# Layer 1's shared weights joined to the scaled mask by an accumulating DMA instead of VectorE

## The chip, the cores and the metric

The kernel runs on one core of a Trainium2 chip, in one launch. The time is device microseconds of the core; five runs of the kernel before gave a median of 629.24 us (628.68 to 630.3). A profile of one further execution of it is shown below.

## The reference

Eight batches of 256 tokens with 1024 features pass four layers, each added to its input. All data is float32, the masks are int32.

```python
# layer 0: a shared weight and a mixture of 8 experts of rank 16 (top 2 of the logits)
base = jnp.einsum('btd,od->bto', x, W)
...
return base + SCALING * lora_out
# layer 1: a shared weight W, a bias, and a signed mask of its own for each batch
output = jnp.einsum('bsi,oi->bso', hidden_states, W) + b
sign = (2 * mask - 1).astype(hidden_states.dtype)
diff = jnp.einsum('bsi,bio->bso', hidden_states, sign)
return output + diff * coeff[:, None, None]
# layer 2: one of 8 full weights, chosen by the batch's adapter
w = weight[adapter_ids]
return jnp.einsum('bsi,boi->bso', x, w)
# layer 3: one of 8 adapters of rank 16
...
x = x + _L0_cond_ref(x, itok_B_0_7, L0_cond_W, L0_cond_Wr, L0_cond_A, L0_cond_B)
x = x + _L1_cond_ref(x, L1_cond_W, L1_cond_b, condB_coeff, mask_Bx4096x4096_ik1)
x = x + _L2_cond_ref(x, L2_cond_weight, itok_B_3_7)
x = x + _L3_cond_ref(x, L3_cond_A, L3_cond_B, itok_B_3_7)
```

What matters here is layer 1. For a batch with coefficient c, its weight is W + c (2 mask - 1), and with the residual W + c (2 mask - 1) + I, where I is the identity. W is the same for all batches, the mask is not.

## The kernel before, in words

**Tiling.** The residual stream is kept transposed, with features on the 128 partitions. A weight of 1024 x 1024 is cut into eight blocks by output feature; a block is a tile of 128 partitions x 1024 elements, 512 KB, and holds all inputs of 128 outputs. Batches go in four pairs, q = 0 to 3. The list `units` is the stream of weight blocks in the order of use: for each pair one block "A" (the experts' first matrix), eight blocks "L0", 16 "L1" (eight outputs m, two batches j) and 16 "L2". So a pair has 41 units.

**Precision.** Each float32 operand is split into two float32r parts, a high and a low one. For a unit of A or L0, `three` multiplies both batches of a pair at once: 24 products of 512 columns (lines 412, 413, 420). For a unit of L1 or L2, `two` multiplies one batch: eight products of the high weight with both parts of x side by side (line 428, 512 columns), and eight of the low weight with the high x (line 436, 256 columns).

**A block's preparation.** `load` brings the block in on SP's queue, `LOAD_AHEAD` = 9 units before its use, into one of `RAW_BUFS` = 10 buffers with the tag "raw" (x's halves and layer 3's matrices take their turn in the same ring). `fold` adds the identity to the 128 x 128 part where inputs and outputs are the same (line 159, VectorE). `prep_hi` casts the block to its high part on ScalarE (line 184), and `prep_lo` subtracts that from the block on VectorE (line 191) for the low part; this happens about `PREP_AHEAD` = 4 units ahead. `LAGS` puts some low parts later around the change from layer 1 to layer 2.

**Layer 1 takes two steps more.** `load` also brings in the shared block w1[m] once for a pair of batches (line 133, a ring of `W1_BUFS` = 3). `merge` turns the int32 mask into 2 c mask - c on ScalarE, in place (line 154). `merge_add` adds the shared block on VectorE (line 174), after having added the identity to the shared block itself (line 159, once for both batches).

**The order of the work is written out by hand.** The program runs `slot(i)` for each unit i. In it: the load of unit i + 9; stores of finished outputs; the evacuation of unit i - 1 from PSUM (ScalarE lines 704, 711, 714; VectorE lines 718, 720); preparation of the units up to i + 4; unit i's products; and at its end the merge for the next slot's `merge_add`. Which unit is merged where stands in `merges`: `MERGE_AHEAD` = (6, 7) units of a pair are merged in the slots before layer 1 (six for the first pair, seven for the others), and the rest are spread over the next 12 slots:

```python
for u in range(2 * K):
    merges[n0 + (u - M if u < M else (u - M) * (2 * K - D) // n)] = n0 + u
```

Each engine runs its instructions in the program's order and waits on semaphores. SP issues all loads and nearly all stores. GpSimd writes a few constants at the start and has nothing to do after that. The products of layers 0 to 2 use four PSUM buffers (tag "mm"), so a buffer is free again only when the evacuation of the unit four earlier is done.

Of the kernel before, what the change touches and what calls it, by code (L numbers as in the profile page):

```python
# [15 lines left out]
P = 128  # L16
NB = 8          # batches
T = 256         # tokens of a batch
K = 8           # blocks of 128 features
E = 8           # experts / adapters  # L20
R = 16          # rank
LOAD_AHEAD = 9  # weight blocks loaded, and prepared, ahead of their products
PREP_AHEAD = 4
MERGE_AHEAD = (6, 7)    # layer 1's blocks merged before the layer: the first pair's, the others'
W1_BUFS = 3
RAW_BUFS = 10
WARM = 9        # products that raise the tensor engine's clock
# prepared later, so that the vector engine is free where layer 2 waits for layer 1's results
# [4 lines left out]
def kernel(ctx: ExitStack, tc: tile.TileContext, x, lang, coeff, ids,  # L33
                           mask, w0, wr, la, lb, w1, b1, w2, a3, b3, out):
    """The residual stream is kept transposed (features on partitions), so that each
    layer's output is the next one's moving operand. float32 operands are split
    exactly into two float32r parts (hi: 12 bits, lo: the rest)."""
# [17 lines left out]
    # ---- small constants  # L55
    xraw = {}

    def load_x(b, h, parts=1):
        """Half of batch b's input."""
        t = rawp.tile([P, K // 2, T], F32, tag="raw", name=f"x{b}_{h}")  # L60
        n = K // 2 // parts
        for i in range(parts):
            c = slice(i * n, (i + 1) * n)
            nc.sync.dma_start(t[:, c, :], x[b, :, h * K // 2 + i * n:h * K // 2 + (i + 1) * n, :])
        xraw[b, h] = t

    # the router's weights: 8 columns and 24 of zeros, a quarter of the array's
# [8 lines left out]
    # the sum over the array's quarters, of R rows each, as three copies  # L76
# [11 lines left out]
    # ---- splits  # L88
# [19 lines left out]
    # ---- the stream of weight blocks, in the order of use  # L108
    units = []
    for q in range(NB // 2):  # L110
        units.append(("A", q, 0, 0))
        units += [("L0", q, m, 0) for m in range(K)]
        units += [("L1", q, m, j) for m in range(K) for j in range(2)]
        order = [(m, j) for m in range(K) for j in range(2)]
        if q == NB // 2 - 1:        # the last pair's first batch ends sooner
            order[-6:] = [(m, j) for j in range(2) for m in range(K - 3, K)]
        units += [("L2", q, m, j) for m, j in order]
    raws, ws, w1raw = {}, {}, {}

    def parts(i):  # L120
        # the first blocks come in two parts
        n = 2 if i < 2 else 1
        return [slice(j * K // n, (j + 1) * K // n) for j in range(n)]

    def load(i):
        if i >= len(units):
            return
        kind, q, m, j = units[i]
        b = 2 * q + j
        if kind == "L1":  # L130
            if j == 0:
                w = rawp.tile([P, K, P], F32, tag="w1", name=f"w1_{q}_{m}", bufs=W1_BUFS)
                nc.sync.dma_start(w, w1[m])
                w1raw[q, m] = w
            t = rawp.tile([P, K, P], I32, tag="raw", name=f"raw{i}")
            nc.sync.dma_start(t, mask[b, m])
        else:
            t = rawp.tile([P, K, P], F32, tag="raw", name=f"raw{i}")
            if kind == "A":
                for c in parts(i):  # L140
                    nc.sync.dma_start(t[:, c], la[:, c])
            elif kind == "L0":
                for c in parts(i):
                    nc.sync.dma_start(t[:, c], w0[m][:, c])
            else:
                src = w2[bass.ds(adapter(b), 1), m]
                nc.sync.dma_start(t, src.rearrange("a p k c -> (a p) k c"))
        raws[i] = t

    # a block's preparation in four steps, on two engines in turns  # L150
# [5 lines left out]

    def add_identity(w, m):
        """The residual, in the block where inputs and outputs are the same."""
        nc.vector.tensor_tensor(w[:, m, :], w[:, m, :], ident, ALU.add)  # L159
# [3 lines left out]
    def fold(i):  # L163
        if i < len(units) and units[i][0] in ("L0", "L2") and i not in folded:
            add_identity(raws[i], units[i][2])
            folded.add(i)

    def merge_add(i):
        if i < len(units) and units[i][0] == "L1":
            s = f32(raws[i])  # L170
            _, q, m, j = units[i]
            if j == 0:
                add_identity(w1raw[q, m], m)
            nc.vector.tensor_tensor(s, s, w1raw[q, m], ALU.add)  # L174
# [28 lines left out]
    # first blocks, ahead of the other constants  # L203
# [26 lines left out]
    def constants():  # L230
        # 5 where the expert is the batch's language; ids below 0 match none
# [8 lines left out]
        # adapters as an index: from the end below 0, then held in range  # L240
# [6 lines left out]
    # ---- layer 0's router, from logits [16 = hi|lo, 512 tokens]  # L247
# [4 lines left out]
    def logits(b, h):  # L252
        """Half of batch b's logits in float32, four blocks of features at a time in the
        quarters of the array."""
        q, j = divmod(b, 2)
        if (j, h) == (0, 0):
            pls[q] = aux.tile([P, 512], F32, tag="aux", name=f"pl{q}")
        for g in range(4):
            nc.tensor.matmul(pls[q][32 * g:32 * g + 32, j * T:(j + 1) * T],  # L259
                             wrs[:, 4 * h + g, :], xraw[b, h][:, g, :],  # L260
                             start=(h == 0), stop=(h == 1))
# [11 lines left out]
    def router(q, pt):  # L273
# [31 lines left out]
        # 2 (the scaling) over 1 + e, and e times that  # L305
# [28 lines left out]
    # ---- layer 3, per batch  # L334
# [20 lines left out]
    def proj_sum(b, pb):  # L355
        """The sum over the quarters, three times."""
        pr = aux.tile([P, 512], F32, tag="aux", name=f"pr{b}")
        if b == NB - 1:
            # in one step, as nothing else is left to do meanwhile
# [13 lines left out]
    def third(b, pb):  # L373
        """The projections' rows as hi, lo and hi again."""
# [21 lines left out]
    # ---- products  # L396
# [11 lines left out]
    def three(po, hi, lo, xhi, xlo, last=True, early=(), mid=(), late=()):  # L408
        """po = (hi + lo)^T (xhi + xlo), over the K blocks of 128; early, mid, late:
        other work in between."""  # L410
# [14 lines left out]
    def two(po, hi, lo, xhl, early=(), mid=(), late=()):  # L425
        """As three(), for one batch: hi with x's both parts at once, into po's halves."""
# [21 lines left out]
    summed = []     # units whose two halves' sum is under way  # L448
    done = []       # what is left of the units that have gone through the tensor engine
# [11 lines left out]
    def proj(b, h):  # L461
        """Half of batch b's projections onto its adapter's rank, in float32 and the
        quarters of the array."""
# [14 lines left out]
    def first_products():  # L478
        """The first two units' products and the first logits, as the input comes in."""
# [20 lines left out]
        for j in range(2):  # L500
# [15 lines left out]
            # both halves stay open, for the experts' part, in one group that batch 0 starts  # L516
# [11 lines left out]
    def main(i):  # L528
        """Unit i on the tensor engine."""
# [12 lines left out]
        elif kind == "L0":  # L542
# [12 lines left out]
            if m == 1:  # L555
                def gate_now():
                    gates[q] = gate(gxs.pop(q), phs.pop(q))
                # the first gates come later than the others
# [15 lines left out]
        else:  # L574
# [21 lines left out]
            if i == len(units) - 1:  # L596
                # its sum is waited for at once
                po = po[:, :T]
                three(po, hi, lo, xh[:, :, 0], xh[:, :, 1])
            else:  # L600
                two(po, hi, lo, xh, early=early, mid=mid, late=late)
# [6 lines left out]
    nxt = []        # work for the vector engine once the scalar engine's is done  # L608

    def side(i):  # L610
        """Other loads and preparations beside unit i's products."""
# [19 lines left out]
    # the tensor engine's clock rises while the first blocks come in  # L631
# [8 lines left out]
    # the slots in which layer 1's weights are merged: the more in layer 0's, which leave the  # L640
    # vector engine time
    merges = {}
    for q in range(NB // 2):
        n0 = units.index(("L1", q, 0, 0))
        M = MERGE_AHEAD[min(q, 1)]
        n = 2 * K - M
        for u in range(2 * K):
            merges[n0 + (u - M if u < M else (u - M) * (2 * K - D) // n)] = n0 + u

    def slot(i):  # L650
        """Unit i's products, beside the evacuation of those before it and the
        preparation of those after it."""
# [4 lines left out]
        bulk = nxt[:]  # L657
        nxt.clear()
        ahead = i + min(D, 2 + max(0, i - 2))
        if i in merges:  # L660
            bulk.insert(0, lambda: merge_add(merges[i]))
        if i > 1:
            bulk = bulk[:1] + [lambda: lows(ahead - lag)] + bulk[1:]
# [3 lines left out]
        # the next products wait for the last ones' results: nothing between  # L667
# [28 lines left out]
    def evacuate(between=None):  # L696
        """Products (and bias) split into the next ones' operand."""
        items = done[:]
        done.clear()
        # those summed beside the last unit, then those complete on PSUM  # L700
# [27 lines left out]
    # the last batch's end: half of the residual joins on the tensor engine, so that two  # L728
    # engines can take the sums
# [81 lines left out]
```

## Time and profile before

| | us |
|---|---|
| median of five runs | 629.24 |
| the profiled execution | 628.82 |
| its span, first to last instruction | 627.0 |
| ScalarE: high parts, line 184, 166 of them | 172.4 |
| ScalarE: evacuations and bias in layer 1, line 714, 64 of them | 30.4 |
| SP's own waits, longest in total: line 147 for VectorE's low parts | 129.9 |
| TensorE's granted clock, mean | 0.997 |

The page gives the busy time of each engine in the span. An engine that is busy for less than the span waits in between, and a list of groups of instructions says for each group what ended the idle time just before it. A second view follows the chain of work that ended last back to the start; 98% of it is TensorE. The windows give busy times in a stretch of the span, so that a stage can be read by itself: a pair of batches takes some 152 us, as the first layer-1 units of the pairs start at about 66.8, 219.2, 371.6 and 524.0 us. The DMA rows give the share of time in which the core's 16 DMA engines were busy and what they moved: 125.01 MB in all, at a mean of 199 GB/s.

### The profile page before, as it was taken

The numbers are of one execution on the slowest core, as the hardware profiler recorded it, in microseconds if no ns is written. First come the engines' busy times: TensorE is split into PE (matmuls) and PEld (weight loads), VectorE is DVE, ScalarE is ACT, GpSimd is POOL, SyncE is SP. The second block draws the span as 40 slices with busy tenths as digits, with TensorE's granted clock in tenths as the row PEclk, the third lists the DMA queues.
The fourth block names the chain that finished last, engine by engine and source line by source line (L and its number), as shares of the span: only waits on it lengthen the run. The fifth ranks groups of instructions, "written<-read, shape, count | busy, mean of one in ns | idle before, by whom it ended". The sixth has DMA issues, their size and how long they took to land.

```text
span 627.0 us, 9247 instructions
## 1 busy us (share of the span) xinstructions
PE 618.7 (99%) x3458; PEld 521.8 (83%) x3458; DVE 460.3 (73%) x800; ACT 362.8 (58%) x552; POOL 1.0 (0%) x14
## 2 busy tenths in 40 slices
PE   8999999999999999999999999999999999999996
PEld 6888888888788888888878888888787888888885
DVE  6685898766657799777666689967775678987642
ACT  5375797465354498655435558865534446975521
POOL 0000000000000000000000000000000000000000
PEclk9999999999999999999999999999999999999998
DMA  8974575567625785376842777547774358754104
GB/s 277 392 225 155 202 269 179 202 214 273 238 71 168 221 282 198 138 251 220 320 125 73 205 234 283 188 139 242 241 269 134 123 181 268 245 193 165 38 0 135
DMA packets 38815, 125.01 MB, mean 199 GB/s; under 512 B 4722, under 2 KB 5874, under 8 KB 38770
## 3 DMA queue, kind: packets, MB, share of 16 engines
q1 hardware_dynamic: 38626, 124.15, 58.4%
q8 instruction: 27, 0.44, 0.3%
q10 hardware_dynamic: 144, 0.26, 0.1%
q14 instruction: 18, 0.15, 0.1%
HBM read 116.01 MB, written 8.39 MB: 198 GB/s over the span
## 4 chain that ended last, share of the span: by engine, by line
PE 98%; DMA 1%; SPq 0%; DVE 0%; ACT 0%; DVEq 0%; issue 0%
PE po L428 37%; PE po L436 20%; PE po L412 9%; PE po L420 9%; PE po L413 9%; PE pb L467 1%; PE po L454 1%; PE po L455 1%; PE po L456 1%; PE pl L259 1%; PE po L388 1%; PE ph L420 1%; PE ph L413 1%; PE ph L412 1%; DMA raw<-in_la 1%; PE ph L489 0%
## 5 line engine op out<-in xcount | busy, mean ns | idle before, releaser
L428 PE MATMUL po<-hl,whi 128*128 128x512 f32 x1016 | 254.5, 392 | 0.0
L428 PEld LDWEIGHTS po<-hl,whi 128*128 128x128 f32 x1016 | 182.9, 189 | 32.9
L191 DVE TENSOR_TENSOR wlo<-raw,whi 128x1024 fp32r<-128x1024 f32 (+1 forms) x166 | 198.9, 1204 | 1.8 <-ACT whi L184 1.8
L184 ACT CAST whi<-raw 128x1024 fp32r<-128x1024 f32 (+1 forms) x166 | 172.4, 1039 | 10.8 <-DVE raw L159 8.4
L436 PEld LDWEIGHTS po<-hl,wlo 128*128 128x128 f32 x1016 | 137.7, 190 | 12.2 <-issue 3.3
L436 PE MATMUL po<-hl,wlo 128*128 128x256 f32 x1016 | 142.7, 283 | 0.0
L412 PE MATMUL po<-x0hi,whi 128*128 128x512 f32 x248 | 97.1, 392 | 0.0
L413 PE MATMUL po<-x0lo,whi 128*128 128x512 f32 x248 | 96.7, 390 | 0.0
L174 DVE TENSOR_TENSOR raw<-raw,w 128x1024 f32<-128x1024 f32 x64 | 78.1, 1220 | 3.6 <-ACT raw L154 2.6
L154 ACT ACTIVATE raw<-raw,negc,c 128x1024 f32<-128x1024 int32 x64 | 79.7, 1245 | 0.0
L711 ACT COPY xt<-po 128x256 f32<-128x256 f32 x63 | 23.4, 372 | 87.2 <-PE po L436 87.2
L720 DVE TENSOR_TENSOR xt<-po,xt 128x256 f32<-128x256 f32 x63 | 26.6, 423 | 50.7 <-ACT xt L711 50.4
L420 PE MATMUL po<-x0hi,wlo 128*128 128x512 f32 x248 | 62.3, 393 | 0.0
L704 ACT CAST hl<-po 128x256 fp32r<-128x256 f32 x64 | 20.5, 376 | 71.6 <-PE po L456 71.5
L718 DVE TENSOR_TENSOR hl<-po,hl 128x256 fp32r<-128x256 f32 x64 | 23.8, 419 | 46.1 <-ACT hl L704 40.8
L412 PEld LDWEIGHTS po<-x0hi,whi 128*128 128x128 f32 x248 | 46.6, 188 | 11.1 <-issue 1.2
L413 PEld LDWEIGHTS po<-x0lo,whi 128*128 128x128 f32 x248 | 46.6, 188 | 9.8
L420 PEld LDWEIGHTS po<-x0hi,wlo 128*128 128x128 f32 x248 | 45.4, 188 | 8.8
L714 ACT ACTIVATE sum<-po,b_sb 128x256 f32<-128x256 f32 x64 | 30.4, 475 | 23.5 <-PE po L436 23.2
L720 DVE TENSOR_TENSOR sum<-po,sum 128x256 f32<-128x256 f32 x64 | 26.8, 419 | 12.7 <-ACT sum L714 12.7
L718 DVE TENSOR_TENSOR hl<-sum,hl 128x256 fp32r<-128x256 f32 x64 | 26.8, 418 | 4.6 <-ACT hl L704 4.6
L704 ACT CAST hl<-sum 128x256 fp32r<-128x256 f32 x64 | 25.6, 400 | 7.5 <-DVE sum L720 7.5
(116 smaller groups left out, 379.5 us busy)
## 6 DMA issues: line engine op xcount, KB each, us to landing
raw<-in_w SPq DMA_DIRECT2D x95, 512.0 KB, 4.3
raw<-in_mask SPq DMA_DIRECT2D x64, 512.0 KB, 5.3
w<-in_w SPq DMA_DIRECT2D x32, 512.0 KB, 4.7
out<-xt SPq DMA_DIRECT2D x31, 256.0 KB, 3.0
x<-in_x SPq DMA_DIRECT2D x12, 512.0 KB, 4.7
a3raw<-in_a SPq DMA_DIRECT2D x8, 384.0 KB, 3.6
x<-in_x SPq DMA_DIRECT2D x8, 256.0 KB, 5.5
raw<-in_la SPq DMA_DIRECT2D x3, 512.0 KB, 3.5
```

The source lines that it names most:

```text
L154: nc.scalar.activation(f32(raws[i]), raws[i], AF.Identity, bias=negc[:, b:b + 1], scale=c2[:, b:b + 1])
L174: nc.vector.tensor_tensor(s, s, w1raw[q, m], ALU.add)
L184: nc.scalar.copy(hi[:, c], source(i)[:, c])
L191: nc.vector.tensor_tensor(lo[:, c], source(i)[:, c], f32(ws[i])[:, c], ALU.subtract)
L412: nc.tensor.matmul(po, hi[:, k, :], xhi[:, k, :], start=(k == 0), stop=False)
L413: nc.tensor.matmul(po, hi[:, k, :], xlo[:, k, :], start=False, stop=False)
L420: nc.tensor.matmul(po, lo[:, k, :], xhi[:, k, :], start=False, stop=(last and k == K - 1))
L428: nc.tensor.matmul(po, hi[:, k, :], xhl[:, k].rearrange("p h t -> p (h t)"), start=(k == 0), stop=False)
L436: nc.tensor.matmul(po[:, :T], lo[:, k, :], xhl[:, k, 0, :], start=False, stop=(k == K - 1))
L704: nc.scalar.copy(hi, p)
L718: nc.vector.tensor_tensor(lo, p, f32(hi), ALU.subtract)
L720: nc.vector.tensor_tensor(xs, p[:, :T], xs, ALU.add)
```

## The change

Layer 1's shared weights are no longer loaded into a ring of their own and added on VectorE. After ScalarE has scaled a mask in place, GpSimd issues a DMA from w1[m] in HBM onto the same tile with `accum_op=ALU.add`; there is one for each batch and block, 64 in all, where before one load served two batches. The tile's identity is then added by `fold` as for the other layers, once for each batch, before the high part is cast. Merges run at a fixed distance: the merge of unit u closes slot u - 9 (`MERGE_AHEAD` = 8, one slot earlier at its end). With the ring of three shared blocks gone, `RAW_BUFS` grows from 10 to 12 and `LOAD_AHEAD` from 9 to 11. On VectorE the low parts keep their place after the evacuation, and the identities of the units five and six ahead come behind them. The diff without changed comments:

```diff
-LOAD_AHEAD = 9
+LOAD_AHEAD = 11
 PREP_AHEAD = 4
-MERGE_AHEAD = (6, 7)
-W1_BUFS = 3
-RAW_BUFS = 10
+MERGE_AHEAD = 8
+RAW_BUFS = 12
...
         if kind == "L1":
-            if j == 0:
-                w = rawp.tile([P, K, P], F32, tag="w1", name=f"w1_{q}_{m}", bufs=W1_BUFS)
-                nc.sync.dma_start(w, w1[m])
-                w1raw[q, m] = w
             t = rawp.tile([P, K, P], I32, tag="raw", name=f"raw{i}")
             nc.sync.dma_start(t, mask[b, m])
...
             nc.scalar.activation(f32(raws[i]), raws[i], AF.Identity,
                                  bias=negc[:, b:b + 1], scale=c2[:, b:b + 1])
+            nc.gpsimd.dma_start(f32(raws[i]), w1[units[i][2]], accum_op=ALU.add)
...
     def fold(i):
-        if i < len(units) and units[i][0] in ("L0", "L2") and i not in folded:
-            add_identity(raws[i], units[i][2])
+        if i < len(units) and units[i][0] != "A" and i not in folded:
+            add_identity(source(i), units[i][2])
             folded.add(i)
-
-    def merge_add(i):
-        if i < len(units) and units[i][0] == "L1":
-            s = f32(raws[i])
-            _, q, m, j = units[i]
-            if j == 0:
-                add_identity(w1raw[q, m], m)
-            nc.vector.tensor_tensor(s, s, w1raw[q, m], ALU.add)
...
-    merges = {}
-    for q in range(NB // 2):
-        n0 = units.index(("L1", q, 0, 0))
-        M = MERGE_AHEAD[min(q, 1)]
-        n = 2 * K - M
-        for u in range(2 * K):
-            merges[n0 + (u - M if u < M else (u - M) * (2 * K - D) // n)] = n0 + u
+    merges = {i - MERGE_AHEAD: i for i, u in enumerate(units) if u[0] == "L1"}
...
         lag = LAGS.get((kind, m, j), 1)
-        bulk = nxt[:]
+        bulk = nxt[:] or [lambda: None]
         nxt.clear()
         ahead = i + min(D, 2 + max(0, i - 2))
-        if i in merges:
-            bulk.insert(0, lambda: merge_add(merges[i]))
         if i > 1:
-            bulk = bulk[:1] + [lambda: lows(ahead - lag)] + bulk[1:]
+            bulk.insert(1, lambda: lows(ahead - lag))
             bulk.append(lambda: fold(ahead + 1))
             if ahead - i == D:
                 bulk.append(lambda: fold(ahead + 2))
```

More of the change, by code (lines that the diff above doesn't have):

```diff
@@ L117 @@
         units += [("L2", q, m, j) for m, j in order]
-    raws, ws, w1raw = {}, {}, {}
+    raws, ws = {}, {}
     def parts(i):
```

## The prediction

> **What bounds the kernel now.** First the page's busy shares and the forty slices:
>
> ```profile
> PE 618.7 (99%) x3458; PEld 521.8 (83%) x3458; DVE 460.3 (73%) x800; ACT 362.8 (58%) x552; POOL 1.0 (0%) x14
> ...
> PE   8999999999999999999999999999999999999996
> ...
> DVE  6685898766657799777666689967775678987642
> ...
> DMA  8974575567625785376842777547774358754104
> GB/s 277 392 225 155 202 269 179 202 214 273 238 71 168 221 282 198 138 251 220 320 125 73 205 234 283 188 139 242 241 269 134 123 181 268 245 193 165 38 0 135
> ```
>
> TensorE is full in all slices but the first and last. As its busy time includes modelled ends, I checked it against the windows by stage and the chain in order of time. Layer 1 of the second pair (219 to 264 us), columns PE, PEld, DVE, ACT, POOL, clock, DMA share, GB/s:
>
> ```profile
> 219.00:264.00 45.00, 45.00 (x260) 39.56 (x259) 39.78 (x65) 36.50 (x56) 0.00 (x0) 1.00 0.63 217
> ```
>
> and the chain there (start, us):
>
> ```profile
> 203.86 1.85 PE po L420 x8
> ...
> 210.52 1.85 PE po L420 x8
> ...
> 219.23 1.83 PE po L428 x8
> 221.06 0.95 PE po L436 x8
> 222.01 1.84 PE po L428 x8
> 223.85 0.95 PE po L436 x8
> 224.80 1.84 PE po L428 x8
> ```
>
> A unit of layer 1 or 2 follows the last after 2.79 us (222.01 to 224.80), one of layer 0 after 6.66 us (203.86 to 210.52), with nothing between. The clock is 1.00. So the products set the time, and preparation counts only where it comes too late for them. Last, the costliest groups and the transfers (KB each, us to landing):
>
> ```profile
> L191 DVE TENSOR_TENSOR wlo<-raw,whi 128x1024 fp32r<-128x1024 f32 (+1 forms) x166 | 198.9, 1204 | 1.8 <-ACT whi L184 1.8
> ...
> L174 DVE TENSOR_TENSOR raw<-raw,w 128x1024 f32<-128x1024 f32 x64 | 78.1, 1220 | 3.6 <-ACT raw L154 2.6
> L154 ACT ACTIVATE raw<-raw,negc,c 128x1024 f32<-128x1024 int32 x64 | 79.7, 1245 | 0.0
> ...
> raw<-in_mask SPq DMA_DIRECT2D x64, 512.0 KB, 5.3
> w<-in_w SPq DMA_DIRECT2D x32, 512.0 KB, 4.7
> ```
>
> **What goes, and what it is worth.** The 64 additions of L174 leave VectorE: 78.1 us. The identity was added to 32 shared blocks and is now added to 64 merged ones: 32 more of L159, whose median is 284 ns, so 9.1 us come back. VectorE falls from 460 to some 391 us. All of it lies beside TensorE, busy 45.00 of 45.00 us in the stage where these additions are; the gain is 0. ScalarE does the same 64 merges. SP issues 32 loads fewer, and its mask loads go two units earlier, into two more buffers; TensorE waits for a load only in the first us of the run (0.3 us for x), so this too is 0. TensorE's 8.3 us of idle time (627.0 - 618.7) lie in the first 19 us and at the last batch's end; every stage between, like the one shown, is full. Nothing is removed at either end. A gain above 0.2% (1.3 us, about what a measurement can tell from no change; smaller differences I call the same) has no place to come from.
>
> **What comes.** 64 transfers of 512 KB (0.524 MB) from GpSimd's queue, against 32 fewer from SP's: net 16.8 MB more read from HBM on 125.0, and each adding transfer must also read the tile that it adds to. GpSimd's queue holds nothing else, so an add that waits there for ScalarE's merge delays only the adds behind it. The new wait that matters is VectorE's: it adds the identity only once the sum has landed, two units before ScalarE splits the block. Behind that instruction, in program order, stand the evacuation of the finished products, which frees their PSUM buffer for TensorE, and the next low parts.
>
> The place is narrow. The merge of unit u closes slot u-9, the identity stands in slot u-6. Nine merges of a pair fall into the slots of A and layer 0, most 6.66 us long, where an add of a few us fits. The other seven fall into layer 1's first seven slots: a train of adds 2.79 us apart, while SP loads one block of 512 KB in each such slot on the same 16 DMA engines.
>
> Price of a load: between 9 and 40 us SP's queue took 96.1% of the engines and moved 10.69 MB, which is 359 GB/s at full share, so 1.46 us for 0.524 MB. The best pieces there moved 418 GB/s, 1.25 us. Price t of an add: no row shows one. From below it is one load, 1.46 us, since the same block comes in. From above it is three passes of it (read the weights, read the tile, write it), 4.38 us. I take two passes, 2.92 us: an add has two operands to read where a load has one, and writing is part of every load's price. How two queues share the engines no row shows either; I let them alternate block by block, so that one add is done every S = t + 1.46 = 4.38 us.
>
> When is the last of the seven too late? Count from the start of layer 1 (219.2). ScalarE ends the merge of that slot 2.8 us later (220.75 + 1.25). The last add lands 7S after that, plus an issue (0.35, as SP's), plus what a landing takes beyond its service (4.4, the median over these tiles, less 1.46 = 2.9): 7S + 6.1. VectorE comes to its identity in slot nine, 9 x 2.79 = 25.1, plus 2.0 (the identity at 260.40 in the slot whose evacuation began at 258.42): 27.1. VectorE may then run late, because four PSUM buffers let TensorE go on until the fourth unit after the one not evacuated: three slots, 8.4, less the 0.9 by which the evacuation normally ends: 7.5. The loss of a pair is 7S + 6.1 - 27.1 - 7.5 = 7S - 28.5, and TensorE begins to wait at S = 4.07. At 4.38 it is 2.2 us, over four pairs 8.6. A second wait follows: by layer 2, whose first products need all of layer 1, VectorE must have caught up. It gains 2.79 - 2.0 = 0.79 us in each of six slots, 4.7 of the 7.5, which leaves 2.8 us a pair, 11 in all. Products that the lags put off later may cover some of it; I take half, 5.6. Together 14 us.
>
> The Trainium skill speaks against the change here: "Collectives: The Full Stack", section "The bandwidth ceiling: the fold count and why AG ≠ RS ≠ AR", says that reducing through these engines runs at about half a copy's rate because each sum pushes two source reads through the same ring, measured 1.93 to 1. By that, as an estimate, t would be 2.82, S 4.28 and the sum 1.5 x 4 + 5.6 = 12 us, near the one above; the trace of before has no adding transfer to test it.
>
> The start: merges begin in slot 0 instead of slot 2, so two of 1.15 us (start to next start) come ahead of the gates' copies on ScalarE. The gates' last part ends at 32.8 and is used at 34.0. I take 0, as ScalarE idles 2.9 us ahead of 27.4 and 1.6 ahead of 31.5; without that cover 32.8 + 2.3 - 34.0 = 1.1 us would be lost, once.
>
> Sum: the profiled run took 628.8 us (a span of 627.0 and 1.8 around it), 0.4 under the median of 629.24. With 14 us more it is 643. The likeliest case's own range is 632 to 651, from just past the break-even to both waits in full at a slightly longer S.
>
> **The rivals.** *Hidden.* The adds end within the cover: S at most 4.07. The place is the train of seven; the point from which it decides is t = 2.61. For it: at the peak of 418 GB/s two reads and a load take 3 x 1.25 = 3.75, and SP's loads may slip, being 11 units ahead of their products. Then the time stays at 629: not slower. Against it: the mean full rate, 359 GB/s, gives 4.38.
>
> *One at a time.* If each add must land before the next one moves, the interval is a landing, 5.3 us as the masks', with no further landing at the end: 2.8 + 0.35 + 7 x 5.3 - 27.1 - 7.5 = 5.6, times four and with the 5.6 of layer 2's start 28 us: 657. Against it: the program lets eight adds be in flight before it waits for one's semaphore.
>
> *Three passes or worse.* t = 4.38, S = 5.84: 12.4 a pair, 50 us and 5.6, 684, and more if descriptors made by software are slow; POOL is busy 1.0 us now, so no row tells. Even then it is still the same place that decides.
>
> *It does not do what it says.* VectorE could keep its load if the sum were waited for at once. It isn't: three slots lie between.
>
> **How the numbers follow.** Two passes 0.43, hidden 0.23, one at a time 0.14, three passes or worse 0.20. Predicted 643. The range takes in hidden, one at a time, and three passes up to its own figure: 628.5 to 685. About half of the last case (0.10) is left out above and 0.03 below. Slower is 0.43 + 0.14 + 0.20 = 0.77, same 0.20 and faster 0.03 out of hidden.
>
> **What would show it.** L174 gone, 64 transfers at GpSimd, VectorE near 391 us. If I am right: TensorE loses its full share in the middle of layer 1, in its last six units and at layer 2's start, and not in layer 0; VectorE's identity at L156 waits for DMA there; landings of adds grow along the train. The rate is wrong if an add's landing stays under 7 us within the train: then the time is unchanged. A wait of TensorE from layer 1's first units on, or in layer 0, would mean that a single add is longer than three slots, and the sum too small.

## The result

| | us |
|---|---|
| before, all 47 runs: median (lowest to highest) | 628.93 (628.47 to 630.96) |
| after, 27 runs | 630.09 (629.15 to 632.45) |
| after, 11 further runs of the same kernel | 630.21 (629.78 to 631.5) |
| after / before | 1.0017, 95% interval 1.001 to 1.0023 |
| after / before, the further runs | 1.0024, 1.0015 to 1.0033 |
| the profiled execution after (span) | 630.6 (628.8) |

The change costs about 1.2 us, or 0.2%: a loss that can be told from nothing, just, and far from the 14 us that I forecast. The time is that of the rival *Hidden*. In 13 of the 65 executions of before that are listed with their clock, the mean granted clock was 0.995 or 0.996 and the time 630.4 to 630.9 us, against 628.5 to 629.7 in the others; without such executions the medians of before and after are 628.9 and 630.0, 1.1 us apart. The profile after, in the same views; first the page's busy shares, two groups and one row of transfers:

```profile
PE 620.0 (99%) x3458; PEld 521.7 (83%) x3458; DVE 395.1 (63%) x768; ACT 361.1 (57%) x552; POOL 56.8 (9%) x78
...
L152 POOL DMA_DIRECT2D raw<-in_w x64 | 55.8, 872 | 492.5 <-DMA a3raw<-in_a 232.7
...
L156 DVE TENSOR_TENSOR raw<-raw,ident 128x128 f32<-128x128 f32 x160 | 45.5, 285 | 48.1 <-DMA raw<-in_w 47.9
...
raw<-in_w POOLq DMA_DIRECT2D x64, 512.0 KB, 8.7
```

VectorE has lost 65.2 us of work (460.3 to 395.1) and gained a wait of 47.9 us at its identity, for the adds. GpSimd issues 64 adds at 0.87 us each, and they land after 8.7 us. TensorE is as full as before (99%). The stage that the prediction argued over, layer 1 of the second pair (columns as in the windows before: PE, PEld, DVE, ACT, POOL, clock, DMA share, GB/s):

```profile
219.00:264.00 45.00, 45.00 (x255) 39.43 (x254) 29.09 (x57) 33.15 (x52) 6.10 (x7) 1.00 0.97 281
```

VectorE fell from 39.78 to 29.09 us there, and the DMA engines went from 0.63 to 0.97. TensorE is busy for the whole window in both. The train of seven adds can be read from VectorE's timeline (start, duration, instruction; in brackets the idle time just before and what ended it). Each late identity is followed by the evacuation (L698, L700) and the low part (L180):

```profile
231.74 0.29 DVE L156 TENSOR_TENSOR raw<-raw,ident 128x128 f32<-128x128 f32 x1 [0.76 <-DMA raw<-in_w]
231.95 0.42 DVE L698 TENSOR_TENSOR hl<-sum,hl 128x256 fp32r<-128x256 f32 x1
232.29 0.41 DVE L700 TENSOR_TENSOR sum<-po,sum 128x256 f32<-128x256 f32 x1
232.62 1.21 DVE L180 TENSOR_TENSOR wlo<-raw,whi 128x1024 fp32r<-128x1024 f32 x1
235.54 0.29 DVE L156 TENSOR_TENSOR raw<-raw,ident 128x128 f32<-128x128 f32 x1 [1.71 <-DMA raw<-in_w]
...
239.36 0.29 DVE L156 TENSOR_TENSOR raw<-raw,ident 128x128 f32<-128x128 f32 x1 [1.73 <-DMA raw<-in_w]
...
250.77 0.29 DVE L156 TENSOR_TENSOR raw<-raw,ident 128x128 f32<-128x128 f32 x1 [1.71 <-DMA raw<-in_w]
...
255.19 0.29 DVE L156 TENSOR_TENSOR raw<-raw,ident 128x128 f32<-128x128 f32 x1 [2.33 <-DMA raw<-in_w]
```

So the predicted mechanism is there, wait for wait. VectorE stands at its identity for seven adds in a row, and one add comes home every 3.80 us (235.54 to 239.36 is 3.82; 239.36 to 250.77 is three times 3.80) where a slot takes 2.79. At 255.19 VectorE is 7.6 us behind: in this execution layer 1 starts 1.28 later than in the profile before, so its identity was due at 219.2 + 1.28 + 27.1 = 247.6. Then the train is over and VectorE catches up. In this pair TensorE never noticed: the four PSUM buffers held out.

To see where the 1.2 us went I took the start of each of the 3458 products in the trace after less that of the same product before. This offset is 0.41 us by 10 us, stays at 0.39 to 0.41 to 100, grows to 1.28 by 120 (0.69 near 103 in the first pair's layer 1, 0.20 where layer 2 starts), is flat to 417, grows by 0.20 where the third pair's layer 2 starts, and ends at 1.48. So part of the loss is in the opening, and part in pairs whose train ended later than 7.6 us. The first pair's late identities and TensorE's waits, from VectorE's timeline and the list of waits of the whole run (PEld is TensorE's weight load; us in total, times, longest):

```profile
86.45 0.29 DVE L156 TENSOR_TENSOR raw<-raw,ident 128x128 f32<-128x128 f32 x1 [1.76 <-DMA raw<-in_w]
91.59 0.29 DVE L156 TENSOR_TENSOR raw<-raw,ident 128x128 f32<-128x128 f32 x1 [3.05 <-DMA raw<-in_w]
...
102.92 0.29 DVE L156 TENSOR_TENSOR raw<-raw,ident 128x128 f32<-128x128 f32 x1 [1.76 <-DMA raw<-in_w]
```

```profile
PEld po L417 <- DVE hl L698: 0.7, 2, 0.4
PEld po L417 <- DVE sum L700: 0.6, 1, 0.6
```

One interval of this train took 5.14 us (86.45 to 91.59). The last identity is 8.6 us late, and TensorE waits in layer 1 for the evacuation (L700) that stands behind it. The two waits for L698 are those at layer 2's start, in the first and the third pair.

### The profile page after: what moved, and what is told of

The parts are those of the page before. It is cut to its first block, busy times and chain, and to the rows that moved or that the text cites. A ratio compares the mean times of both kernels' runs of the same rounds, so it can differ in the third digit from the quotient of the medians.

```text
span 628.8 us, 9412 instructions
## 1 busy us (share of the span) xinstructions
PE 620.0 (99%) x3458; PEld 521.7 (83%) x3458; DVE 395.1 (63%) x768; ACT 361.1 (57%) x552; POOL 56.8 (9%) x78
## 3 DMA queue, kind: packets, MB, share of 16 engines
q0 software_dynamic: 9216, 33.56, 28.1%
## 4 chain that ended last, share of the span: by engine, by line
PE 82%; issue 7%; DMA 6%; DVE 1%; POOL 1%; SPq 0%; ACT 0%; DVEq 0%; POOLq 0%; ACTq 0%
PE po L417 33%; PE po L425 18%; PE po L401 7%; PE po L409 7%; PE po L402 7%; DMA raw<-in_w 3%; DMA raw<-in_mask 2%; PE pb L456 1%; PE po L377 1%; PE ph L409 1%; DMA x<-in_x 1%; PE po L443 1%; PE pl L248 1%; PE po L444 1%; PE po L445 1%
## 5 line engine op out<-in xcount | busy, mean ns | idle before, releaser
L180 DVE TENSOR_TENSOR wlo<-raw,whi 128x1024 fp32r<-128x1024 f32 (+1 forms) x166 | 198.9, 1203 | 5.0 <-PE po L409 2.8
L152 POOL DMA_DIRECT2D raw<-in_w x64 | 55.8, 872 | 492.5 <-DMA a3raw<-in_a 232.7
L156 DVE TENSOR_TENSOR raw<-raw,ident 128x128 f32<-128x128 f32 x160 | 45.5, 285 | 48.1 <-DMA raw<-in_w 47.9
L698 DVE TENSOR_TENSOR hl<-po,hl 128x256 fp32r<-128x256 f32 x64 | 23.8, 419 | 62.2 <-ACT hl L684 56.9
L700 DVE TENSOR_TENSOR xt<-po,xt 128x256 f32<-128x256 f32 x63 | 26.6, 422 | 48.7 <-ACT xt L691 48.2
L401 PEld LDWEIGHTS po<-x0hi,whi 128*128 128x128 f32 x248 | 46.6, 188 | 11.1 <-issue 1.2
L698 DVE TENSOR_TENSOR hl<-sum,hl 128x256 fp32r<-128x256 f32 x64 | 26.8, 419 | 7.1 <-ACT hl L684 7.1
```

The lines of the kernel that those rows point to most:

```text
L152: nc.gpsimd.dma_start(f32(raws[i]), w1[units[i][2]], accum_op=ALU.add)
L180: nc.vector.tensor_tensor(lo[:, c], source(i)[:, c], f32(ws[i])[:, c], ALU.subtract)
L401: nc.tensor.matmul(po, hi[:, k, :], xhi[:, k, :], start=(k == 0), stop=False)
L698: nc.vector.tensor_tensor(lo, p, f32(hi), ALU.subtract)
```

## The experiments

Ten runs follow, nine of them of other kernels and one of the kernel after again, each compared with the kernel before on the same chip. The theory at their start: S, the interval of the adds, is set by the DMA engines and lies just inside the cover; loss comes only where the train runs out of it. The rivals changed from run to run and stand in the expectations.

### Without the adds

```diff
-            nc.gpsimd.dma_start(f32(raws[i]), w1[units[i][2]], accum_op=ALU.add)
```

> The 64 adding transfers are left out, and with them layer 1's shared weights. Theory 1 (the 1.2 us of the changed kernel come from the adds in the first pair's train): the time is that of the kernel before, 628.9, and the DMA share in layer 1 of the second pair falls from 0.97 to some 0.4. Theory 2 (the 1.2 us come from the other edits: the longer ring, earlier loads, identities and merges): the time stays at 630.1.

Measured: 629.59 us (628.82 to 630.91), ratio 1.0014, interval 1.0005 to 1.0024. So the adds are not the whole of the 1.2 us. The offset of the products is 0.22 us by 20 us, 0.64 from 38 us on, and then flat to the end: no train, no loss in any layer 1. The DMA share from 219 to 264 us falls from 0.97 to 0.54. Of the 0.64, 0.42 falls near 34 us, at the first pair's gates (the high and low copies of layer 0's gated expert terms).

### Copies in place of the adds

```diff
-            nc.gpsimd.dma_start(f32(raws[i]), w1[units[i][2]], accum_op=ALU.add)
+            nc.gpsimd.dma_start(f32(raws[i]), w1[units[i][2]])
```

> The same 64 transfers from GpSimd's queue, but as plain copies over the scaled mask, which so drops out of the result. Theory 1 (an add costs two reads): the queue's share of 16 engines falls from 28.1% (2.76 us for each transfer) to about 15% (1.46 us), landings in the train fall from 11 to 5 us, and the time is 628.9. Theory 2 (the price lies in descriptors made by software or in the queue, not in adding): the share stays near 28%, and the time near 630.1.

Measured: 629.59 us (629.01 to 631.22), ratio 1.0008, 0.9998 to 1.0019: not to be told from before by its time. The kernel after's transfers between 219 and 250 us (queue, packets, MB, share of 16 engines; then KB each and us to landing), and behind them GpSimd's queue over its whole span:

```profile
q0 software_dynamic: 1021, 3.73, 60.6%
q1 hardware_dynamic: 1410, 5.13, 44.2%
...
raw<-in_w POOLq DMA_DIRECT2D x7, 512.0 KB, 11.1
```

```profile
q0 software_dynamic: 9216, 33.56, 28.1%
```

The same with copies, between 219 and 250 us and over the whole span:

```profile
raw<-in_w POOLq DMA_DIRECT2D x7, 512.0 KB, 5.1
```

```profile
q0 software_dynamic: 9216, 33.56, 15.5%
```

Over the whole span, GpSimd's queue takes 28.1% of the engines with adds and 15.5% with copies of the same 33.56 MB: 0.281 x 628.8 / 64 = 2.76 us of all 16 engines for an add, 0.155 x 627.9 / 64 = 1.52 for a copy, 1.8 to 1. An add costs nearly two loads, and the landing doubles (5.1 to 11.1 us) while the two queues' shares add up to more than all of the engines (60.6 and 44.2%). With copies, VectorE's identity waits for nothing, though SP's loads and the merges are the same:

```profile
L156 DVE TENSOR_TENSOR raw<-raw,ident 128x128 f32<-128x128 f32 x160 | 45.5, 285 | 0.0
```

GpSimd's issue is longer too with the operation in it: 872 ns against 534 with copies.

### Eight and nine adds in the train

```diff
-MERGE_AHEAD = 8
+MERGE_AHEAD = 7
```

> The merges come one slot later, so that the train in layer 1 has eight adds instead of seven. Theory 1 (the cover ends where n adds of 3.80 us pass 28.5 us): 8 x 3.80 - 28.5 = 1.9 us lost in each pair, 630.1 + 8 = 638, at most 11 more where layer 2 begins. Theory 2 (the prediction's cover was too small, and the adds are far from the products): 630, no change.

and the same with 6:

> Two slots later, nine adds in the train. Theory 1: 9 x 3.80 - 28.5 = 5.7 us in each pair, 630.1 + 23 = 653, at most 11 more. Theory 2: 630 to 633.

Measured: 643.29 us with 7 (642.0 to 643.88; ratio 1.0221, 1.0205 to 1.0236), and with 6 four executions of 657.67, 664.62, 666.18 and 670.17 us at granted clocks of 0.997, 0.991, 0.988 and 0.982 (ratio without the last 1.0538, 1.0485 to 1.0591). At a clock of 0.997 or 0.998 both are 5 us above the sums by S alone, 638 and 653; what the other executions with 6 take beyond that goes with their lower clock. With 7, TensorE's loss sits at the last units of layer 1 (the windows' columns as above), by the list of waits behind VectorE's evacuations, and the interval is still 3.80:

```profile
249.00:264.00 15.00, 12.85 (x70) 10.74 (x70) 8.20 (x16) 7.78 (x14) 0.87 (x1) 1.00 0.97 273
```

```profile
PEld po L417 <- DVE sum L700: 2.8, 3, 1.0
```

```profile
239.22 0.29 DVE L156 TENSOR_TENSOR raw<-raw,ident 128x128 f32<-128x128 f32 x1 [1.72 <-DMA raw<-in_w]
243.02 0.29 DVE L156 TENSOR_TENSOR raw<-raw,ident 128x128 f32<-128x128 f32 x1 [1.71 <-DMA raw<-in_w]
```

### How late the train may end

These runs give the cover as a number. For each pair I take the last identity that waited for an add, less the time at which it was due (27.1 us after layer 1's start in that execution, which is the start before plus the offset there), and beside it TensorE's loss: the growth of the offset over the pair's layers 1 and 2.

| kernel, pair | last late identity, us | late by | loss | late by - loss |
|---|---|---|---|---|
| after, first | 102.92 | 8.63 | 0.89 | 7.74 |
| after, second | 255.19 | 7.61 | 0.00 | |
| after, third | 407.93 | 7.95 | 0.20 | 7.75 |
| after, fourth | 560.16 | 7.58 | 0.00 | |
| one merge later, first | 106.52 | 11.77 | 4.03 | 7.74 |
| one merge later, second | 262.08 | 10.90 | 3.15 | 7.75 |
| one merge later, third | 417.93 | 11.20 | 3.46 | 7.74 |
| one merge later, fourth | 573.56 | 10.97 | 3.23 | 7.74 |

The cover is 7.74 us in all six pairs that lost anything, and every microsecond beyond it is lost once. The loss has two places, though. In layer 1, TensorE loses what the lateness exceeds 7.94 us by: 0.69 us in the kernel after's first pair, nothing in its third, 2.95 to 3.83 with the merges one later. At layer 2's start, whose first unit needs the last of layer 1's evacuations, it loses another 0.20 in each of the six. Between the last late identity and that place VectorE has six slots; it took 10.52 us for them in the first pair after (103.13 to 113.65), where TensorE's six take 16.74, so it made up 6.2 us:

```profile
103.13 0.42 DVE L698 TENSOR_TENSOR hl<-sum,hl 128x256 fp32r<-128x256 f32 x1
...
113.65 0.42 DVE L698 TENSOR_TENSOR hl<-sum,hl 128x256 fp32r<-128x256 f32 x1 [0.27 <-ACT hl L684]
```

That is more than 0.79 a slot, because two of the six hold no low part (`LAGS`) and take 1.22 and 1.23 us instead of 2.0. The kernel after lives at that edge: in this trace its trains end between 0.9 us past the 7.74 and 0.2 short of them. This table is worked out after the runs, from numbers that no expectation named.

### Is the interval the engines' or the queue's?

The prediction took up to eight adds to be in flight. By GpSimd's timeline after it is three: then GpSimd issues the next only when VectorE's identity three units back has run:

```profile
235.83 0.86 POOL L152 DMA_DIRECT2D raw<-in_w  x1 [2.93 <-DVE raw L156]
```

A queue with room for three would give an interval of its own: a landing of 11.1 and an issue, divided by three, is near 4 as well. So I gave GpSimd's descriptors four times the room, in the kernel with eight adds in the train and then in the kernel after:

```diff
-                   dynamic_dma_scratch_size=1024)
+                   dynamic_dma_scratch_size=4096)
```

> The kernel with eight adds in the train (643.3), with four times the space for GpSimd's descriptors. Theory 1 (the interval of 3.80 us is the DMA engines' rate: three blocks of 0.524 MB, the load's and the add's two, at 414 GB/s): the interval and the time stay, 643. Theory 2 (only three adds fit in flight, and three share a landing of 11.4 us): with more in flight the interval falls below 3.5 us, and the time to some 630 to 633.

> The changed kernel with the same larger space. Theory 1: 630.1, as without it. Theory 2: the first pair's wait goes, 629.6 as without the adds.

Measured: 644.47 us with eight adds (642.94 to 646.26; ratio 1.0224, 1.0199 to 1.025), against 643.29 with the small room (the two of its four executions with a granted clock of 0.999 took 642.94 and 642.96); and 630.04 for the kernel after (629.25 to 632.17; 1.0008, 0.9997 to 1.0019). GpSimd now runs ahead, a slot apart (here in the kernel after):

```profile
235.34 0.86 POOL L152 DMA_DIRECT2D raw<-in_w  x1 [1.69 <-ACT hl L684]
238.13 0.88 POOL L152 DMA_DIRECT2D raw<-in_w  x1 [1.93 <-ACT hl L684]
```

but in the second pair of both kernels the train's identities stay 3.76 to 3.85 us apart once it is under way, and the later adds just wait longer in the queue (from issue at 238.13 to the identity at 251.85 for the sixth, where it was 239.64 to 250.77 with the small room). The interval is the engines'. If an add counts as two reads, they read three times 0.524 MB in 3.80 us (weights and tile for the add, one block for SP), 414 GB/s: near the best pieces of the opening (418), not its mean of 359.

### The start

```diff
-    merges = {i - MERGE_AHEAD: i for i, u in enumerate(units) if u[0] == "L1"}
+    merges = {}
+    for i, u in enumerate(units):
+        if u[0] == "L1":
+            late = {9: 3, 10: 3, 11: 4}.get(i, i - MERGE_AHEAD)
+            merges.setdefault(late, []).append(i)
...
         if i + 1 in merges:
-            merge(merges[i + 1])
+            for u in merges[i + 1]:
+                merge(u)
```

> The changed kernel, but the first pair's first three merges stand behind the gates on ScalarE. Theory 1 (two merges ahead of the gates cost about 0.4 us of TensorE's time at 34 us): 629.6, and the gates' last part ends before 33.5 us. Theory 2 (what is lost without the adds is lost elsewhere): 630.1.

Measured: 629.69 us (629.17 to 631.3), ratio 1.0004, 0.9994 to 1.0014, near theory 1's 629.6; but its runs scatter over 2 us, so the place is read from the traces. In the kernel with copies, the gates' last part on VectorE and then TensorE's product with it:

```profile
33.68 0.69 DVE L90 TENSOR_TENSOR glo<-gt,ghi 128x512 fp32r<-128x512 f32 x1 [0.69 <-ACT ghi L89]
```

```profile
34.42 0.50 PE L444 MATMUL po<-glo,lb 128*128 128x512 f32 x1 [0.20 <-DVE glo L90]
```

In the kernel with the merges behind the gates:

```profile
32.52 0.69 DVE L90 TENSOR_TENSOR glo<-gt,ghi 128x512 fp32r<-128x512 f32 x1 [0.69 <-ACT ghi L89]
```

With two merges ahead of them, the gates' last copy ends at 34.4, 1.5 us later than before (32.8), and TensorE waits; with the merges behind them it ends at 33.2, well ahead of its use at 34.4, and TensorE doesn't. In the kernel after's own first trace the copy ends at 34.25, and as TensorE is 0.41 us late there already, it loses nothing at this place. Then the trains, too: the same, with a train of six.

```diff
-            late = {9: 3, 10: 3, 11: 4}.get(i, i - MERGE_AHEAD)
+            early = 2 * u[2] + u[3] > 5
+            late = {9: 3, 10: 3, 11: 4}.get(i, i - MERGE_AHEAD - early)
```

> The same, and the merges from the seventh of a pair on one slot earlier, two of them in one slot of layer 0, so that the train in layer 1 has six adds. Theory 1 (both causes add up, the gates' 0.4 us and the first pair's 0.6 us): the time of the kernel before, 628.8 to 629.1. Theory 2 (neither): 630.

Measured: 629.78 us (628.93 to 631.46), ratio 1.0002, 0.9991 to 1.0014. The last late identities are 3.1 to 4.7 us late instead of 7.3 to 8.6, and neither kernel loses anything after 10 us. Their times can't be told from each other or from the kernel before, so neither theory's figure is confirmed, and nothing beats before.

### The kernel after, again

> The kernel after once more, unchanged. Two small losses were read in its first profile: 0.3 to 0.4 us at about 34 us, where the first products of layer 0 wait for the gates' copies, and 0.6 us between 86 and 103 us, where the first pair's train holds up VectorE. Theory 1 (both belong to the kernel): TensorE is again less than full in the window from 66 to 111 us, by 0.3 us or more, and the ratio to before is again 1.001 to 1.002. Theory 2 (the loss in the first pair is one execution's accident, as the margin there is some tenths of a microsecond): TensorE is full in that window, and what remains of the difference lies ahead of 40 us.

Measured: 630.21 us, ratio 1.0024, 1.0015 to 1.0033. In this profile TensorE is busy 45.00 of 45.00 us from 66 to 111, and the trains end 7.3 to 7.8 late: losses of 0, 0, 0.09 and 0.03 us. The offset is 0.43 by 10 us, 0.56 after the gates and 0.68 at the end. So theory 2 holds for the place of the loss: the 0.9 us of the first profile was one execution's long interval. But the ratio is again above 1.001, as theory 1 had it, and the profiled execution is the fastest of the eleven (629.78), so what the median execution loses, and where, no trace shows. What makes one interval of a train 5.1 us instead of 3.8 I don't know; the engines were no slower in it, as the two queues moved 0.70 and 0.67 MB from 86.45 to 91.59 us, and 0.53 and 0.52 in the 3.85 us before.

### The due time moved

```diff
-MERGE_AHEAD = 8
+MERGE_AHEAD = 7
...
             bulk.append(lambda: fold(ahead + 1))
-            if ahead - i == D:
-                bulk.append(lambda: fold(ahead + 2))
```

> Eight adds in the train, as in the run that took 643.3, but VectorE's identity moves one slot later (five units ahead of the products and not six; the line that folds the unit six ahead is left out). Theory 1 (the loss is the wait of VectorE at its identity, which holds up the evacuations queued behind it): the due time moves by one slot of 2.79 us, so the loss of a pair is 8 x 3.80 - 28.5 - 2.79 = -0.9, and the time falls to 629 to 632. Theory 2 (what is late is the block itself, for ScalarE's high part or for the products, and the place of the identity does not count): the time stays at 643.

Measured: 639.88 us (638.48 to 640.33), ratio 1.0169, 1.0155 to 1.0182, between the two. The due time counts, but moving it by 2.79 us saved only 0.5 to 2.0 us a pair: the losses are 2.08, 2.33, 2.13 and 2.72. Taken against the new due time (29.9), the last identities are 8.5 to 9.1 us late, and late less loss is 6.40 in all four pairs, 1.34 less than 7.74. In layer 1 nothing has changed: the losses there are 0.53, 0.79, 0.59 and 1.17, and late less these is 7.93 or 7.94, as before. So theory 1 holds in layer 1. What it left out is layer 2's start, which now costs 1.54 us in each pair instead of 0.20. From the list of waits from 219 to 275 us:

```profile
ACT whi L173 <- DVE raw L156: 11.3, 11, 2.1
...
PEld po L417 <- DVE hl L696: 1.7, 1, 1.7
```

VectorE has one slot less in which to catch up, and the identity now stands so close ahead of ScalarE's high part of the same block that ScalarE waits as well, with its own evacuations behind. In the first pair:

```profile
107.19 0.42 DVE L696 TENSOR_TENSOR hl<-sum,hl 128x256 fp32r<-128x256 f32 x1
...
116.25 0.42 DVE L696 TENSOR_TENSOR hl<-sum,hl 128x256 fp32r<-128x256 f32 x1 [0.55 <-ACT hl L682]
```

Five slots in 9.06 us instead of 13.95 make up 4.9 us, 1.3 less than the 6.2 above, which is what layer 2's start costs more. Of it, 0.8 is the missing slot; the rest is in the two short slots, where VectorE waits 0.55 us for ScalarE instead of 0.27.

## Why the prediction was wrong

I forecast a loss of 14 us and there was one of 1.2; what happened was *Hidden*, to which I had given 0.23. The waits that I named are all there; two terms of the sum were mis-sized, S and with it the first wait (8.6 us forecast), and the second wait at layer 2 (5.6). Step by step:

- **The gain, taken as 0: right.** VectorE gave up 65 us (69 were forecast; it lands at 395, not 391), and nothing was earned, in the kernels without a train either.
- **Price of the add, t = 2.92: near.** It took 2.76 us of the engines. The Trainium skill ("Collectives: The Full Stack", "The bandwidth ceiling: the fold count and why AG ≠ RS ≠ AR") has 1.93 to 1 between a collective that copies and one that reduces; here, with an adding load from HBM against the same load as a copy, it is 1.8 to 1.
- **S = t + load = 4.38: this step failed.** One add and one load do alternate, but in 3.80 us, not 4.38. I had priced each pass by the mean rate of a stretch whose pieces ran from 63 to 423 GB/s (359 at full share), while many of them already showed 418. Under two full queues the engines keep nearly that up: 414, an add counted as two reads. The break-even was 4.07, so this one rate decided whether TensorE waits for the train in every pair. The rival had it written out: "at the peak of 418 GB/s two reads and a load take 3 x 1.25 = 3.75".
- **The last landing.** By S = 3.80 the formula puts it at 7 x 3.80 + 6.1 = 32.7 us after layer 1's start; measured 255.19 - 220.48 = 34.7. GpSimd's issue starts 0.4 us after the merge and takes 0.86, where I had 0.35 in all (+0.9). The first landing fits (7.2 measured from the issue's end, 4.38 + 2.9 = 7.3 forecast). The six intervals after it average 3.91, as the last took 4.42. In the lateness, the longer issue took back 0.9 of the 2.8 that these intervals saved: 9.7 was forecast, 7.6 came.
- **Cover 7.5: right**, 7.94 measured in layer 1 and 7.74 in all. Its trains end 7.6 to 8.6 us late, so without the four buffers the kernel after would lose about that in each pair.
- **The second wait at layer 2, half of 11 us: there, but a seventh of its size.** It is 0.20 us in a pair that used up the cover, where 1.4 was forecast (2.8 less half), and 0.4 us in all in the kernel after's first trace. I had VectorE gain 0.79 us in each of six slots, 4.7 in all; it gained 6.2, as `LAGS` takes the low part out of two of them. With a slot less, and ScalarE made to wait too, the wait was 1.54 us a pair.
- **The start, taken as 0: wrong by up to half a microsecond.** I trusted ScalarE's idle time ahead of 27.4 and 31.5. The merge at 27.4 waited 2.5 us for its mask, so the idle time was used up by a DMA wait and the gates' copies slid by 1.5 us.
- **The sign I named for a wrong rate was itself wrong.** I wrote that landings under 7 us in the train would mean an unchanged time. They took 11 us and the time hardly changed: a landing grows with the queue ahead of it, and only the interval tells the rate.

**What the 1.2 us is.** The gates' copies are shown: TensorE can wait there with the two merges ahead and not with them behind, 0.4 to 0.5 us without adds or with copies, 0.0 and 0.1 in the kernel after's two traces, where the opening was late already. The trains past the cover are shown in traces, with their 0.20 at layer 2: 1.1 us in one execution and 0.1 in another. An offset of 0.1 to 2.2 us within the first 20 us, where the input lands, is in every trace taken after the change. Where it is 1.8 us or more, the granted clock from 8 to 20 us is 0.86 in place of 1.00, and that stretch adds 1.0 to 1.5 us of it. In the kernel after's two traces the 0.4 us are there by 8 us, on a wait for x, and until 16 us SP issues the same transfers in the same order in both kernels. There is only one trace of before to set it against, so whether it belongs to the change stays open.

## What to carry to other kernels

An accumulating DMA took nearly two loads of the DMA engines here, so count its interval in passes at the rate that full engines reach, and hold it against the time of one slot times the number of buffers that let the bound engine run on. Then ask whether the late engine can catch up before the next stage needs all of its results. Taking work from VectorE, which stood beside a full TensorE, earned nothing here: it bought 65 us of VectorE's time with a place where one adding transfer more in each train costs 13 us. And idle time just ahead of a critical instruction is cover only if no transfer can arrive in it late: look at what ends that idle time.

## What had not been expected of the hardware

- The busy shares of two queues on the same 16 engines add up to more than the whole (60.6 and 44.2% from 219 to 250 us), so a sum of each one's engine time (2.65 + 1.40 us with seven adds' worth of packets, by 31 x 0.606 / 7.09 and 31 x 0.442 / 9.79) is longer than the 3.80 us that a pair of transfers took.
- GpSimd's issue of one transfer depends on its operation: 872 ns with the addition, 534 without, against 0.33 us for SP's issue of a mask in the same trace.
- Four times the descriptor room let GpSimd run ahead but moved the time by nothing that can be told: 644.47 against 643.29, and 630.04 against 630.09.
